# Masked attention with residual norms on one core: the other work of each step cut into smaller pieces and ordered by due date, with one output bank

## The chip, the cores and the metric

The kernel runs on one core of a Trainium2 chip, as one launch. The metric is the device time of that launch in microseconds. The core's engines are TensorE (PE in the profile), VectorE (DVE), ScalarE (ACT), GpSimd (POOL) and SyncE (SP), which here only issues DMAs. Each engine works through its own instructions in order and waits for the others by semaphores.

## The reference

There are eight frames of 2048 rows and 256 channels, one 0/1 matrix `adj` of 2048 x 2048 for all of them, and 8 heads of 32 channels:

```python
q, k, v = split(x @ w_qkv)                       # per frame: 2048 x 256 each, 8 heads of 32
scores = where(adj > 0, q @ k.T / sqrt(32), -1e9)
t = softmax(scores) @ v
y = layernorm(x + t)
z = layernorm(y + relu(y @ w1 + b1) @ w2 + b2)
out = layernorm(x + z)
```

Everything is float32.

## The kernel before, in words

The scores are held transposed: 128 keys on the partitions, queries along the free dimension. Work is cut into **items** `(f, qc, g, mb)`: frame f of 8, query chunk qc of 4 (512 queries), group g of 2 (4 heads), key block mb of 16 (128 keys). There are 1024 items, 128 in a frame, and 16 successive ones with the same `(f, qc, g)` form a group that sums into one output bank.

The main loop (L535) takes one **step** for each item t. In a step it issues, in this order: other work (`advance`, L449), the exponentials of item t+1 on ACT (L229), the scores of item t+2 (L222: four heads side by side in the rows of PE's array) with the addition of the mask on VectorE (L225, two halves of 128 x 1024), the values of item t (L241: four heads side by side in the columns), and the sum over keys (`add_up`, L256). The scores use three pairs of PSUM banks in turn, two pairs an item. The exponentials of a group are added up for the softmax's denominator: two chains of items by accumulating DMAs that POOL issues (L260; items 1, 4, 7, 10 and 2, 5, 9, 12), the rest by additions on POOL (L263), item 14 alone. POOL waits in its queue until the DMA before in the same chain has landed.

Two further banks, `x0` and `x1`, are left. Before the change they swap roles with each group: one takes the group's output, the other is the only bank for **other work**. This is everything on PE that isn't scores or values, written as generators:

- `turn`: load a chunk of the next frame's rows, transpose it, store it to a DRAM tile `xd`, and make its queries.
- `project`: reload such a chunk and make its keys and its values for one g.
- `denominator`: sum the four terms over the partitions (L299), transpose the result, take its reciprocal.
- `outcome`, then `tail`: divide the output and add x; normalize (`norm`: statistics on VectorE, a power on POOL that yields `nb`, and the scaling on ACT, L281), feed forward (two transposed banks, w1, w2), normalize, add x, normalize, store.

A generator yields `BANK` when it wants the other bank, `MORE` between the two halves of what it puts there, `HOLD` to be continued in the next step, or a number of steps to wait. `advance` continues the holder of the bank by one half a step, or gives the bank to the entry of `fill` with the earliest due step. If another entry is late, or in a group's last step, the holder runs on to its end. In a group's first step nothing of this is done. The table `NEXT` (L475) says in which step of a frame `turn` and `project` of the next frame are started. The reloads come through three tiles named `in`, by DMAs in SP's queue. A piece of `in_columns` with 512 columns (L53) is 8 instructions on PE.

Of the kernel before, what the change touches and what calls it, by code (L numbers as in the profile page):

```python
# [29 lines left out]
BANK, MORE, HOLD, TURNED, ROOM, INPUTS = -1, -2, -3, -4, -5, -10  # L30
# [30 lines left out]
def fast_path(ctx, tc, cst, x, adj, out, RS):  # L61
# [8 lines left out]
    kp = ctx.enter_context(tc.tile_pool(name="kp", bufs=2 * NCK + 2))  # L70
    qp = ctx.enter_context(tc.tile_pool(name="qp", bufs=2 * NCK + 2))
    vp = ctx.enter_context(tc.tile_pool(name="vp", bufs=2 * NCK + 2))
# [12 lines left out]
    state = {"pair": 0, "side": None, "turn": 0, "turned": False, "holder": None, "tails": 0}  # L85
# [65 lines left out]
    def turn_rows(xc, xT):  # L151
        for a in range(2):
            yield BANK
            ps = bank()
            for j in range(TPC):
                nc.tensor.transpose(ps[:, j * P:(j + 1) * P], xc[:, j, a * P:(a + 1) * P], ident)
            nc.scalar.copy(xT[:, a, :], ps)


    def turn(f, c):  # L160
        yield INPUTS - 2
        xc, xT = take([P, TPC, C], F32), take([P, 2, CH], F32)
        nc.sync.dma_start(xc, x[f, c * CH:(c + 1) * CH, :].rearrange("(j p) c -> p j c", p=P))
        yield 3
        yield from turn_rows(xc, xT)
        give(xc)
        yield 1
        nc.sync.dma_start(XD[f][c], xT)
        XT[f, c] = xT
        yield from queries(f, c, xT)  # L170
        give(xT)

    def channels(store, pool, name, key, xT, k0):
        yield BANK
        ps = bank()
        for a in range(2):
            if a:
                yield MORE
            in_columns(nc, ps, wqkv[:, a, k0:k0 + P], xT[:, a, :], start=(a == 0), stop=(a == 1))
        store[key] = pool.tile([P, CH], F32, name=name)  # L180
        nc.scalar.copy(store[key], ps)  # L181

    def reload(f, c):
        while (f, c) not in XT:
            yield 1
        yield INPUTS - 1
        xT = take([P, 2, CH], F32)
        nc.sync.dma_start(xT, XD[f][c])
        yield 3
        return xT  # L190

    def project(f, c, g, xT=None):
# [7 lines left out]
        for j in range(TPC):  # L200
            if j == TPC // 2:
                yield MORE
            for a in range(2):
                in_columns(nc, ps[:, j * P:(j + 1) * P], xT[:, a, j * P:(j + 1) * P],
                           wqkv[:, a, 2 * C + g * P:2 * C + (g + 1) * P], start=(a == 0), stop=(a == 1))
# [81 lines left out]
    def denominator(f, qc, g):  # L287
# [6 lines left out]
        for n, term in enumerate(terms):  # L294
            if n == 2:
                yield HOLD
# [8 lines left out]
        for j in range(TPC):  # L305
            nc.tensor.transpose(ps[:, j * P:(j + 1) * P], dT[:, j::TPC], ident)
# [21 lines left out]
    def divide(f, qc, y):  # L328
        rc = RC.pop((f, qc))
        for gg in range(2):  # L330
# [3 lines left out]
            for j in range(TPC):  # L334
                nc.tensor.transpose(ps[:, j * P:(j + 1) * P], oT[:, j::TPC], ident)
# [57 lines left out]
    def feed_forward(y):  # L393
# [3 lines left out]
        for a in range(2):  # L397
            yield BANK
            ps = bank()
            for j in range(TPC):  # L400
                nc.tensor.transpose(ps[:, j * P:(j + 1) * P], y[:, j, a * P:(a + 1) * P], ident)
# [6 lines left out]
        for d in range(2):  # L408
            yield BANK
            ps = bank()  # L410
            for a in range(2):
                if a:
                    yield MORE
                in_columns(nc, ps, w1s[:, a, d * P:(d + 1) * P], yT[:, a, :], start=(a == 0), stop=(a == 1))
# [4 lines left out]
        for jj in range(0, TPC, 2):  # L419
            yield BANK  # L420
            ps = bank()
            for j in range(jj, jj + 2):
                if j > jj:
                    yield MORE
                for d in range(2):
                    in_columns(nc, ps[:, (j - jj) * C:(j - jj + 1) * C], hT[:, d, j * P:(j + 1) * P], w2s[:, d, :],
                               start=(d == 0), stop=(d == 1))
# [13 lines left out]
    def resume(e, t):  # L441
        e[2] = next(e[1], None)
        state["holder"] = e if e[2] in (MORE, HOLD) else None if state["holder"] is e else state["holder"]
# [5 lines left out]
    def advance(t, free=True, finish=False):  # L449
        inputs = True  # L450
        if state["holder"]:
            free = False
            resume(state["holder"], t)
        for e in list(fill):
            while e[2] is not None and e[0] <= t and e is not state["holder"]:
                if e[2] == BANK:
                    if not free:
# [9 lines left out]
        late = any(e[2] == BANK and e[0] <= t for e in fill)  # L467
        while state["holder"] and (finish or late and state["holder"][2] == MORE):
            resume(state["holder"], t)

    items = [(f, qc, g, mb) for f in range(F) for qc in range(NCK) for g in range(2) for mb in range(MB)]
    LEAD = 2


    NEXT = {(1, 1): [(turn, 0)], (3, 1): [(turn, 1)], (3, 10): [(project, 0, 0)], (5, 1): [(turn, 2)],  # L475
            (5, 8): [(project, 1, 0)], (6, 0): [(turn, 3)], (6, 4): [(project, 2, 0)], (6, 8): [(project, 3, 0)],
            (6, 12): [(project, 0, 1)], (7, 0): [(project, 1, 1)], (7, 4): [(project, 2, 1)], (7, 8): [(project, 3, 1)]}

# [46 lines left out]
    def ask(f, c):  # L525
        xT = yield from reload(f, c)
        yield from queries(f, c, xT)
        give(xT)

    for _ in begin():  # L530
        pass
    for c in range(1, NCK):
        start(0, ask(0, c), 2 * MB * c - LEAD - 1)
    state["side"] = 0
    for t, (f, qc, g, mb) in enumerate(items):  # L535
        if mb == 0 and t:
            state["side"] = 1 - state["side"]
        if g == 1 and mb % 2 and (f + 1 < F or qc + 1 < NCK):
            load_mask(f + (qc + 1) // NCK, (qc + 1) % NCK, mb // 2)
        if f + 1 < F:  # L540
            for what, *which in NEXT.get((2 * qc + g, mb), []):
                due = t + MB // 2 if what is turn else items.index((f + 1, 0, which[1], which[0] * TPC)) - LEAD - 1
                start(t, what(f + 1, *which), due)
# [3 lines left out]
        if mb:  # L547
            advance(t, finish=mb == LAST)
# [12 lines left out]
        if mb == LAST:  # L561
            start(t + SUM, denominator(f, qc, g), t)
# [241 lines left out]
```

## Time and profile before

| | us |
|---|---|
| median of 3 runs | 3399.78 (3391.83 to 3401.1) |
| the profiled execution | 3399.32 |
| its span, first to last instruction | 3397.4 |
| PE busy | 3133.4 |
| POOL busy | 2595.8 |
| DVE busy | 2736.3 |
| ACT busy | 2431.0 |
| first exponentials of the main loop start at | 63.5 |

The mean granted clock of TensorE is 0.981 of full speed. Busy time is the time in which at least one instruction of the engine runs; for PE it is modelled, so that a busy PE need not be at its peak. In a line of the timeline stand the start in us, the duration, the engine, the line of the program, the operation, what it writes and reads, the number of instructions, and in brackets the idle time of the engine before it with what ended it. In a table of windows stand the window, its length, and for each engine its busy time with the number of instructions, then the granted clock and the DMA engines' busy share with what they moved in GB/s. In a list of waits stand who waited for whom, the sum, how often, and the longest.

### The profile page before, as it was taken

What the parts mean: (1) busy time and instruction counts of PE and PEld (TensorE: products, weight loads), DVE (VectorE), ACT (ScalarE), POOL (GpSimd) and SP (SyncE); (2) the same over time, 40 slices, a digit from 0 to 9 for tenths busy, and PEclk for the clock granted to TensorE, in tenths of its full rate; (3) what the DMA queues carried; (4) which work ended last, traced back from release to release, by engine and by line L of the source; (5) the groups of instructions that cost most, each with busy time, mean ns of one, the idle gap of its engine ahead of it and who ended that gap; (6) DMA issues with size and microseconds to landing.
All of it is one profiled execution on the core that took longest, in us unless ns stands there. A gap on an engine that the chain in (4) does not pass through costs nothing. (4 is left out here: it accounts for less than half of the span.)

```text
span 3397.4 us, 68228 instructions
## 1 busy us (share of the span) xinstructions
PE 3133.4 (92%) x28948; PEld 978.7 (29%) x28948; DVE 2736.3 (81%) x3203; ACT 2431.0 (72%) x1937; POOL 2595.8 (76%) x1357
## 2 busy tenths in 40 slices
PE   7899999989999999989999999999999989998884
PEld 4222233222332223222332223322233222332221
DVE  4788878878788887878888788887888877888884
ACT  3677777767677777777777677777777767777773
POOL 0577778787787877877878787887887877788884
PEclk8899999999999999999999999999999999999997
DMA  9678778778688787778787778778788778777773
GB/s 309 141 162 179 167 175 183 156 151 201 149 179 172 160 182 175 169 148 187 171 174 169 159 173 191 152 168 177 166 185 174 157 159 181 175 164 160 160 151 82
DMA packets 149352, 576.88 MB, mean 170 GB/s; under 512 B 14608, under 2 KB 67344, under 8 KB 99888
## 3 DMA queue, kind: packets, MB, share of 16 engines
q0 software_dynamic: 64560, 435.85, 63.9%
q1 hardware_dynamic: 83664, 135.30, 11.9%
q8 instruction: 229, 3.75, 0.4%
q10 hardware_dynamic: 816, 1.31, 0.1%
q14 instruction: 83, 0.68, 0.1%
HBM read 131.99 MB, written 37.75 MB: 50 GB/s over the span
## 5 line engine op out<-in xcount | busy, mean ns | idle before, releaser
L225 DVE TENSOR_TENSOR p<-s,mask 128x1024 f32<-128x1024 f32 x2048 | 2410.1, 1218 | 530.6 <-PE s L222 331.6
L229 ACT ACTIVATE p<-p 128x2048 f32<-128x2048 f32 x1024 | 1956.2, 1910 | 517.8 <-DVE p L225 438.1
L263 POOL TENSOR_TENSOR p<-p 128x2048 f32<-128x2048 f32 x382 | 1828.0, 4806 | 245.4 <-ACT p L229 240.2
L222 PE MATMUL s<-qT,kT 32*128 32x512 f32 x8192 | 1176.3, 644 | 133.2 <-DVE p L225 127.6
L241 PE MATMUL x<-p,v 128*32 128x512 f32 x8192 | 1096.8, 607 | 23.7 <-ACT p L229 23.7
L260 POOL DMA_DIRECT2D p<-p x384 | 364.3, 1016 | 443.7 <-DMA p<-p 241.2
L222 PEld LDWEIGHTS s<-qT,kT 32*128 32x128 f32 x8192 | 321.8, 184 | 774.8 <-DVE p L225 724.2
L241 PEld LDWEIGHTS x<-p,v 128*32 128x32 f32 x8192 | 161.6, 108 | 807.5 <-issue 287.9
L53 PE MATMUL x<-in,wqkv 128*32 128x512 f32 x1888 | 242.5, 603 | 29.9 <-DMA in<-xd 29.0
L281 ACT ACTIVATE y<-y,nb,rs 128x256 f32<-128x256 f32 x372 | 219.4, 591 | 61.8 <-POOL nb L278 61.8
L299 PE MATMUL x<-p,ones 128*32 128x512 f32 x2016 | 239.3, 592 | 0.0
L270 DVE BATCH_NORM_STATS2 st<-y 128x6 f32<-128x256 f32 x372 | 155.2, 417 | 6.3 <-DMA y<-in_x_dram 6.3
L53 PE MATMUL x<-turned,w1s 128*32 128x512 f32 x992 | 123.2, 603 | 5.0 <-ACT hT L415 4.9
L301 ACT COPY dT<-x 128x512 f32<-128x512 f32 x63 | 36.9, 585 | 125.6 <-PE x L299 125.6
L53 PE MATMUL x<-w2s,hT 128*32 128x256 f32 x2048 | 123.8, 382 | 0.4 <-ACT hT L415 0.4
L53 PEld LDWEIGHTS x<-wqkv,in 128*32 128x32 f32 x3584 | 101.0, 110 | 46.1 <-issue 31.4
L53 PEld LDWEIGHTS x<-in,wqkv 128*32 128x32 f32 x1888 | 61.3, 111 | 176.0 <-issue 149.5
L53 PE MATMUL x<-wqkv,in 128*32 128x128 f32 x3584 | 111.9, 273 | 0.0
L299 PEld LDWEIGHTS x<-p,ones 128*32 128x32 f32 x2016 | 65.5, 110 | 150.8 <-issue 150.8
L275 POOL TENSOR_TENSOR rs<-rs,mhalf 128x4 f32<-128x4 f32 x93 | 97.1, 1044 | 7.7
L53 PEld LDWEIGHTS x<-w2s,hT 128*32 128x32 f32 x2048 | 67.0, 111 | 73.2 <-issue 37.5
L181 ACT COPY kT<-x 128x512 f32<-128x512 f32 x59 | 34.5, 585 | 73.3 <-PE x L53 72.7
(117 smaller groups left out, 1421.5 us busy)
## 6 DMA issues: line engine op xcount, KB each, us to landing
p<-p POOLq DMA_DIRECT2D x384, 1024.0 KB, 10.4
mask<-md SPq DMA_DIRECT2D x248, 128.0 KB, 7.3
y<-in_x_dram POOLq DMA_DIRECT2D x62, 512.0 KB, 5.8
in<-xd SPq DMA_DIRECT2D x59, 512.0 KB, 10.7
p<-in_adj_dram SPq DMA_DIRECT2D x16, 1024.0 KB, 9.7
out_dram<-y SPq DMA_DIRECT2D x31, 512.0 KB, 2.9
in<-in_x_dram SPq DMA_DIRECT2D x29, 512.0 KB, 9.1
xd<-in SPq DMA_DIRECT2D x28, 512.0 KB, 8.4
```

Of the source, the lines that this page charges most:

```text
L53: nc.tensor.matmul(out[r:r + D], lhsT[:, r:r + D], rhs, start=start, stop=stop)
L222: nc.tensor.matmul(ps2[half][:, j, :], KT[f, mb // TPC, g][r:r + D, (mb % TPC) * P:(mb % TPC + 1) * P], QT[f, qc, g][r:r + D, :], start=Tr ...
L225: nc.vector.tensor_tensor(pt[:, 2 * half:2 * half + 2, :], ps, MK[f, qc, mb // 2][:, mb % 2, None, :].to_broadcast([P, 2, CH]), ALU.add)
L229: nc.scalar.activation(PT[item], PT[item], AF.Exp, scale=1.0 / math.sqrt(D))
L241: nc.tensor.matmul(O[grp][r:r + D, :], V[f, mb // TPC, g][:, mb % TPC, r:r + D], PT[item][:, h, :], start=(mb == 0), stop=(mb == LAST))
L260: nc.gpsimd.dma_start(PT[f, qc, g, chain[0]], PT.pop(item), accum_op=ALU.add)
L263: nc.gpsimd.tensor_tensor(first, first, PT.pop(item), ALU.add)
L270: nc.vector.bn_stats(st, t[:, j, :])
L275: nc.gpsimd.tensor_tensor(rs, rs, cst["mhalf"], ALU.pow)
L281: nc.scalar.activation(t[:, j, :], t[:, j, :], AF.Identity, bias=nb[:, j:j + 1], scale=rs[:, j:j + 1])
L299: nc.tensor.matmul(ps[r:r + D, :], cst["ones"], term[:, h, :], start=(n == 0), stop=(n == len(terms) - 1))
L301: nc.scalar.copy(dT, ps)
```

## The change

Other work is metered. Each call of `advance` adds a credit of 2200, kept at most at 2200, and each piece takes 4 for each of its columns (2048 for 512 columns), a transposed bank 1400. A piece is issued if at least 1024 are left, or if the earliest entry that could use the bank is due. The halves become smaller: values yield `MORE` after each of four column blocks, the denominator after each of its four terms. The forced end in a group's last step and the rest in its first step are dropped. `WAIT` replaces `HOLD`: the denominator starts two steps after its group instead of four, but its last term is held until the fourth.

Queries are no longer made in `turn`. A generator `ask` reloads the chunk and makes them, for the same frame in steps 2, 34 and 66 (chunks 1 to 3) and for the next frame's chunk 0 in step 66. The other entries of `NEXT` move too, and reloads wait five steps instead of three before they are used. There are 12 tiles for keys and for values instead of 10, and 6 for queries instead of 10. `state["side"]` stays 0: output always goes to `x0`, and other work to `x1`.

```diff
-BANK, MORE, HOLD, TURNED, ROOM, INPUTS = -1, -2, -3, -4, -5, -10
+BANK, MORE, WAIT, TURNED, ROOM, INPUTS = -1, -2, -3, -4, -5, -10
+STEP, UNIT, TURN, KEPT = 2200, 1024, 1400, 2200
...
-    kp = ctx.enter_context(tc.tile_pool(name="kp", bufs=2 * NCK + 2))
-    qp = ctx.enter_context(tc.tile_pool(name="qp", bufs=2 * NCK + 2))
-    vp = ctx.enter_context(tc.tile_pool(name="vp", bufs=2 * NCK + 2))
+    kp = ctx.enter_context(tc.tile_pool(name="kp", bufs=3 * NCK))
+    qp = ctx.enter_context(tc.tile_pool(name="qp", bufs=6))
+    vp = ctx.enter_context(tc.tile_pool(name="vp", bufs=3 * NCK))
...
+    def columns(out, lhsT, rhs, start, stop):
+        state["credit"] -= 4 * out.shape[-1]
+        in_columns(nc, out, lhsT, rhs, start, stop)
+
+    def transposes(ps, src, ident=ident):
+        state["credit"] -= TURN
+        for j, s in enumerate(src):
+            nc.tensor.transpose(ps[:, j * P:(j + 1) * P], s, ident)
...
         nc.sync.dma_start(xc, x[f, c * CH:(c + 1) * CH, :].rearrange("(j p) c -> p j c", p=P))
-        yield 3
+        yield 5
         yield from turn_rows(xc, xT)
         give(xc)
         yield 1
         nc.sync.dma_start(XD[f][c], xT)
         XT[f, c] = xT
-        yield from queries(f, c, xT)
         give(xT)
...
         nc.sync.dma_start(xT, XD[f][c])
-        yield 3
+        yield 5
         return xT
...
         for j in range(TPC):
-            if j == TPC // 2:
+            if j:
                 yield MORE
...
         for n, term in enumerate(terms):
-            if n == 2:
-                yield HOLD
+            if n:
+                yield MORE
+            while n == len(terms) - 1 and state["now"] < ready:
+                yield WAIT
+            state["credit"] -= 4 * CH
...
-    def advance(t, free=True, finish=False):
+    def advance(t, finish=False):
+        state["credit"] = min(max(state["credit"], 0) + STEP, KEPT)
+        state["now"] = t
+        free = not state["holder"]
+
+        def more():
+            if state["holder"] and state["holder"][2] == WAIT:
+                return False
+            due = [e[3] for e in fill if e[2] == BANK and e[0] <= t or e is state["holder"]]
+            return finish or state["credit"] >= UNIT or min(due) <= t
+
+        if state["holder"]:
+            resume(state["holder"], t)
+            while state["holder"] and more():
+                resume(state["holder"], t)
         inputs = True
-        if state["holder"]:
-            free = False
-            resume(state["holder"], t)
         for e in list(fill):
             while e[2] is not None and e[0] <= t and e is not state["holder"]:
                 if e[2] == BANK:
-                    if not free:
+                    if not free or not more():
                         break
...
-        late = any(e[2] == BANK and e[0] <= t for e in fill)
-        while state["holder"] and (finish or late and state["holder"][2] == MORE):
-            resume(state["holder"], t)
+            while e is state["holder"] and more():
+                resume(e, t)
...
-    NEXT = {(1, 1): [(turn, 0)], (3, 1): [(turn, 1)], (3, 10): [(project, 0, 0)], (5, 1): [(turn, 2)],
-            (5, 8): [(project, 1, 0)], (6, 0): [(turn, 3)], (6, 4): [(project, 2, 0)], (6, 8): [(project, 3, 0)],
-            (6, 12): [(project, 0, 1)], (7, 0): [(project, 1, 1)], (7, 4): [(project, 2, 1)], (7, 8): [(project, 3, 1)]}
+    NEXT = {1: [(turn, 0)], 2: [(ask, 1)], 20: [(turn, 1)], 34: [(ask, 2)], 40: [(project, 0, 0)], 50: [(turn, 2)],
+            60: [(project, 1, 0)], 66: [(ask, 0), (ask, 3)], 72: [(turn, 3)], 80: [(project, 2, 0)], 92: [(project, 3, 0)],
+            100: [(project, 0, 1)], 104: [(project, 1, 1)], 108: [(project, 2, 1)], 112: [(project, 3, 1)]}
...
-    for c in range(1, NCK):
-        start(0, ask(0, c), 2 * MB * c - LEAD - 1)
     state["side"] = 0
     for t, (f, qc, g, mb) in enumerate(items):
-        if mb == 0 and t:
-            state["side"] = 1 - state["side"]
...
-        if mb:
-            advance(t, finish=mb == LAST)
+        if t:
+            advance(t)
...
         if mb == LAST:
-            start(t + SUM, denominator(f, qc, g), t)
+            start(t + 2, denominator(f, qc, g, t + SUM), t + SUM + 4)
```

The calls of `in_columns` and the loops of transposes in the generators now go through `columns` and `transposes`.

## The prediction

> **What bounds the kernel now.** I read the page first (busy shares), then the timeline in two ordinary stretches, then the table of windows over one of the eight frames, then the list of waits. The page:
>
> ```profile
> PE 3133.4 (92%) x28948; PEld 978.7 (29%) x28948; DVE 2736.3 (81%) x3203; ACT 2431.0 (72%) x1937; POOL 2595.8 (76%) x1357
> ```
>
> No engine is far from full, so the average settles nothing. I went to the timeline, where the first score matmul (L222) of each step is the clock tick. First without other work between values (L241) and the next scores, then with one piece (L53, x8) and with two (x16); of the lines, only PE's are shown:
>
> ```profile
> 1450.59 1.14 PE L222 MATMUL s<-qT,kT 32*128 32x512 f32 x8 [0.35 <-DVE p L225]
> 1451.65 1.07 PE L241 MATMUL x<-p,v 128*32 128x512 f32 x8
> ...
> 1453.13 1.14 PE L222 MATMUL s<-qT,kT 32*128 32x512 f32 x8 [0.41 <-DVE p L225]
> ```
>
> ```profile
> 1606.61 1.14 PE L222 MATMUL s<-qT,kT 32*128 32x512 f32 x8
> ...
> 1608.57 1.04 PE L53 MATMUL x<-in,wqkv 128*32 128x512 f32 x8
> ...
> 1609.54 1.14 PE L222 MATMUL s<-qT,kT 32*128 32x512 f32 x8
> ...
> 1611.49 1.90 PE L53 MATMUL x<-turned,w1s 128*32 128x512 f32 x16
> ...
> 1613.32 1.14 PE L222 MATMUL s<-qT,kT 32*128 32x512 f32 x8
> ```
>
> The empty step takes 2.54 us and PE waits 0.35 to 0.41 us in it for VectorE; one piece takes 2.93 us, two take 3.78 us, both without a gap on PE. So a step is bound by the larger of two things: a loop of VectorE's first half and the scores (about 2.5 us), or PE's own sum: scores 1.07, values 1.00 and 0.86 a piece. I took the distance between first score matmuls for 1020 of the 1024 steps and sorted them by the other work on PE in between: empty, median 2.55 us; one transposed bank 2.75; one piece 2.93; two pieces 3.78. These four medians times their counts give 3113.6 us of the 3223.4 us that the steps take. The missing 109.8 us are stalls in a few places. The windows of frame 3 (its 16-step groups) show one:
>
> ```profile
> 1361.94:1409.33 47.39, 46.56 (x424) 14.18 (x420) 40.79 (x51) 39.05 (x33) 39.11 (x24) 1.00 0.78 170
> ...
> 1458.23:1515.79 57.56, 48.54 (x373) 13.06 (x373) 42.82 (x52) 38.34 (x31) 45.91 (x26) 0.94 0.83 179
> ```
>
> The first group has PE busy 46.56 of 47.39 us; the second loses about 9 us and TensorE's granted clock falls to 0.94. The timeline there, and the waits:
>
> ```profile
> 1506.43 1.94 PE L53 MATMUL x<-in,wqkv 128*32 128x512 f32 x8 [7.24 <-DMA in<-xd]
> 1508.29 1.93 PE L222 MATMUL s<-qT,kT 32*128 32x512 f32 x8
> ```
>
> ```profile
> POOL p L260 <- DMA p<-p: 241.2, 63, 8.1
> ...
> ACT y L281 <- POOL nb L278: 61.8, 20, 9.4
> ```
>
> PE waits in its own queue for a reloaded tile, and runs the next 3.9 us at half pace. The last wait is the other kind: ScalarE, in order, stands behind POOL, which itself waits for an accumulating DMA.
>
> **The Trainium skill.** "Perfetto Trace Analysis", section Optimization Strategy: where the most-contended engine changes over time, interleaving the regimes can help. The trace agrees that there are two regimes, VectorE's 2.55 us and PE's 3.78 us. The same page, section Matmuls: independent matmul groups should rotate through PSUM banks so that an eviction overlaps the next group; the change goes against it for the output bank, priced below. "TensorE: Matmul & The Clock Gate", Part 1: PE falls to half clock after an idle window of about 3.4 us; the 1.93 us scores after 7.24 us of idling, against 1.14, agree. The same page, Architectural detail: ScalarE and VectorE are strict FIFO, which the wait for nb shows.
>
> **The change, part by part.**
>
> Spreading. From the order in which both programs issue PE's instructions I counted the steps by kind (1023 steps). Before: 245 empty, 243 with a transposed bank, 226 with one piece, 309 with two. After: 63, 243, 590, 127. The 844 pieces are the same work (226 + 618 = 590 + 254). So 182 empty steps and 182 double ones become 364 single ones: 182 x (2.55 + 3.78 - 2 x 2.93) = 182 x 0.47 = 85.5 us. PE's idle time in an empty step hides about half of a piece (2.55 + 0.86 would be 3.41, and it is 2.93); that is all there is to win here. Doubles remain because the feed-forward pieces (w1, w2) are past their due step when they get their turn. The steps then cost 3113.6 - 85.5 = 3028.1 us.
>
> Earlier loads. Before, the reload planned in step 58 is first read in step 61, 3 steps of about 2.9 us, while such a reload took 10.7 us at the median and 21.6 at most. Steps 61 and 62 are over their medians by 2.0, 2.4, 6.1, 9.1, 8.1, 6.5 and 8.0 us in frames 0 to 6: 42.2 us. After, I counted from load to first read at least 5 steps (105 to 110) and otherwise 6 to 28, 15 us and more. I take the 42.2 us as gone. If only half of a late load is covered, 20 us stay.
>
> Late queries. Each of the 32 chunks but the very first is now reloaded for its queries, where 3 were before: 28 loads of 512 KB more, each 0.3 to 1.2 us of issue on SP, which only issues and mostly waits. By the page SP's queue moved 135.3 MB in 11.9% of the DMA engines' time, so 14.7 MB more are 1.3%, on top of 78%. Nothing waits for these but the queries, which load 10 steps ahead or more; that lead hides them, and without it each would cost what step 61 did, about 6 us. I take 0, from 0 to 20. Behind a load in SP's queue stand the mask pieces; their next reading is over ten steps away.
>
> Buffers. Keys and values get 12 tiles, queries 6: 30 in all as before. A key tile written in step 111 falls on one that was last read in step 97. Nothing.
>
> One output bank. values' first matmul of a group now waits for the copy oT of the group before; behind it on PE stand the other work and the scores of the step after, and behind those VectorE. In the trace oT ended 0.66 to 2.22 us after the last values matmul (mostly 0.87 to 1.44). The next values follow 1.93 us after it where a piece lies between (0.86 + 1.07), and about 1.43 us where none does (groups starting at steps 48 and 80). So most groups wait nothing; at worst 2.22 - 1.43 = 0.8 us in all 64, 51 us; nothing can be gained by it. I take 0.1 us, 6 us. On the other side the first step of a group, never used for other work before, is now used; that is in the counts.
>
> Denominators. They begin two steps after the group instead of four, one term a step; a chain's sum is read one step earlier, the pool's sum in the same step. Before, PE never waited there (idle before L299: 0.0). In frame 3 POOL issues the last chained add 14 or 15 steps into the group, and it lands 10.4 us (3.5 steps) later, against a reading in step 19: half a step to a step and a half of slack. A wait there holds up PE in order, so the next scores. 0 to 1 us in 64 groups; I take 0.
>
> Less slack. 286 of the 590 single steps also carry VectorE work, mostly the statistics of 0.42 + 0.18 us: 2.36 + 0.60 makes 2.96 to 2.99 us against 2.93. Up to 0.06 x 286 = 17 us, hidden by the steps without; I take 8. The other 67.6 us of stalls (y's division on VectorE about 0.7 us four times a frame, nb about 3 us a frame) I leave as they are, from 30 to 110.
>
> The sum: 3028.1 + 67.6 + 6 + 8 = 3109.7 us of steps, plus 174.0 us outside them (3397.4 - 3223.4, start-up and end, unchanged): span 3283.7 us. The profiled execution took 1.9 us over its span and the median of the runs lies 0.5 us above it: 3286 us, 3.4% below 3399.8. A difference of 0.3% is about what a measurement of this kernel can tell from none.
>
> **Rivals.**
> (1) All scattered stalls shrink too, since nb is now issued in step 60 instead of 61, 90 instead of 92 and 121 instead of 124, with one chained add fewer ahead of it on POOL: 3028 + 25 + 174 + 2 = 3229 us. For it: the 61.8 us of waits behind nb. Against it: POOL has less idle time.
> (2) VectorE or ScalarE becomes the bound. If each step paid its largest engine sum without any help from its neighbours (VectorE 2.40 plus its extras, ScalarE 1.95 plus its extras, PE as above), the steps would take 3167 us: 3343 us. Against it: by the same rule the steps before would take 3268 us and took 3223 with the load stalls.
> (3) Slower: POOL takes over. A group of frame 3 holds 325.5 / 8 = 40.7 us of POOL work, and 241.2 / 64 = 3.8 us of waiting for chained DMAs, 44.5 in all, against 48.4 us a group in my sum. Steps of 3.0 us instead of 3.2 bring a chain's adds 0.6 us closer, four waits a group: 46.9. It decides from 50.4 us a group (3223 / 64), that is, if the waits grow to 9.7 us; at 10 us it is 64 x 50.7 + 174 + 2 = 3421 us. Against it: the group of 47.39 us above ran with 39.11 us of POOL work and no stall, and frame 7 keeps 47 us for several groups.
> (4) The spread does not reach the path: only the loads' 42 us come back, 3357 us. The gapless 2.93 and 3.78 us steps speak against it.
>
> **How the numbers follow.** Sum as worked 0.60 (3255 to 3315), rival 1 0.15, rivals 2 and 4 0.14, rival 3 0.08, no change to speak of 0.03. The range takes the first, most of rival 1 and half of 2: 3232 to 3345 us. Faster 0.88, same 0.03, slower 0.09.
>
> **What would show it.** Right: distances of first score matmuls with the same medians and the new counts; PE busy near 96%; the wait of L53 for the reload gone; granted clock 0.99. Wrong: single steps over 3.05 us at the median; idle time before the denominator's matmuls; values waiting for oT; longer waits behind nb or for chained DMAs on POOL.

## The result, and the profile after

The changed kernel takes 3281.12 us (median of 4 runs, 3279.45 to 3283.31), 0.9656 of the kernel before, with a 95% interval of 0.9639 to 0.9673. The forecast was 3286 us. The profiled execution took 3279.45 us with a span of 3277.3 us, at a mean granted clock of 0.983 (before: 0.981). In the changed kernel the line numbers move: scores L230, mask L233, exponentials L237, values L249, chained DMAs L268, POOL's additions L271, nb L286, the scaling of y L289, denominators L310, pieces of `in_columns` L54.

The first part of the page, busy time by engine:

```profile
PE 3112.2 (95%) x28948; PEld 979.2 (30%) x28948; DVE 2737.7 (84%) x3203; ACT 2438.8 (74%) x1937; POOL 2591.2 (79%) x1357
```

Every engine has the number of instructions it had before, so nothing was taken out. The span is 120 us shorter: PE is idle for 99 us less, and its busy time is 21 us shorter. The timeline of three steps with one piece each, PE's lines only:

```profile
1282.97 1.14 PE L230 MATMUL s<-qT,kT 32*128 32x512 f32 x8
1284.04 1.07 PE L249 MATMUL x<-p,v 128*32 128x512 f32 x8
1284.92 1.04 PE L54 MATMUL x<-in,wqkv 128*32 128x512 f32 x8
1285.89 1.14 PE L230 MATMUL s<-qT,kT 32*128 32x512 f32 x8
1286.97 1.06 PE L249 MATMUL x<-p,v 128*32 128x512 f32 x8
1287.85 1.04 PE L54 MATMUL x<-in,wqkv 128*32 128x512 f32 x8
1288.82 1.14 PE L230 MATMUL s<-qT,kT 32*128 32x512 f32 x8
```

The two halves that the kernel before put into one step of 3.78 us stand in two steps of 2.93 us, without a gap on PE. Sorted as in the prediction (distances of first score matmuls, here over the same 1021 steps of both traces; the sums take the four medians of the kernel before for both kernels):

| steps | before: count, median us | after: count, median us |
|---|---|---|
| without other work | 245, 2.55 | 63, 2.54 |
| one transposed bank | 243, 2.75 | 243, 2.74 |
| one piece | 225, 2.93 | 588, 2.93 |
| two pieces | 308, 3.78 | 127, 3.79 |
| sum of medians | 3116.5 | 3031.8 |
| stalls over the medians | 109.8 | 75.9 |
| outside the steps | 171.1 | 169.6 |
| span | 3397.4 | 3277.3 |

So the span fell by 84.7 us from the kinds of steps, 33.9 from stalls, and 1.5 outside them. The windows of frame 3 of the changed kernel, its fourth group (in which the kernel before lost about 9 us to the reload) and its last:

```profile
1404.13:1449.47 45.34, 44.86 (x408) 13.67 (x404) 41.73 (x52) 35.65 (x29) 36.41 (x23) 1.00 0.95 221
...
1596.08:1647.74 51.66, 48.79 (x481) 15.39 (x477) 42.30 (x52) 39.47 (x33) 44.38 (x26) 0.97 0.88 203
```

The last group in the kernel before:

```profile
1666.66:1718.49 51.83, 50.72 (x509) 16.04 (x509) 42.89 (x52) 38.88 (x33) 42.77 (x25) 1.00 0.82 188
```

The fourth group is now nearly gapless on PE, at full clock. The last has PE idle for 2.9 us, 1.1 before, and a lower clock: a stall that the kernel before did not have there. The list of groups and the list of waits of the changed kernel show what went and what came:

```profile
L249 PE MATMUL x<-p,v 128*32 128x512 f32 x8192 | 1097.6, 608 | 14.0 <-ACT p L237 14.0
...
L310 PE MATMUL x<-p,ones 128*32 128x512 f32 x2016 | 262.8, 598 | 4.3 <-POOL p L271 2.7 <-DMA p<-p 1.6
L54 PE MATMUL x<-in,wqkv 128*32 128x512 f32 x1888 | 244.0, 594 | 4.0 <-DMA in<-xd 4.0
```

```profile
POOL p L268 <- DMA p<-p: 94.4, 36, 6.1
...
DVE p L233 <- DMA p<-p: 49.0, 35, 3.1
...
ACT y L289 <- POOL nb L286: 37.1, 10, 9.3
```

Two lines from the list of waits of the kernel before:

```profile
PE x L53 <- DMA in<-xd: 29.0, 8, 7.2
...
DVE p L225 <- DMA p<-p: 13.6, 9, 3.1
```

PE's wait for a reload fell from 29.0 to 4.0 us (one wait, at step 112 of frame 0). Values never wait for the output's copy `oT`. POOL's own waits for chained DMAs fell from 241.2 to 94.4 us, ScalarE's behind nb from 61.8 to 37.1 us. What grew is VectorE's wait for a p tile that a chained DMA still holds: 49.0 us, 13.6 before. Of the 49.0 us, 33 stand at steps 23, 81 and 115. The timeline at step 115 of frame 3, VectorE's and PE's lines:

```profile
1607.70 1.04 PE L310 MATMUL x<-p,ones 128*32 128x512 f32 x8
1609.55 2.36 DVE L233 TENSOR_TENSOR p<-s,mask 128x1024 f32<-128x1024 f32 x2 [2.30 <-DMA p<-p]
1610.83 1.29 PE L230 MATMUL s<-qT,kT 32*128 32x512 f32 x8 [2.09 <-DVE p L233]
...
1612.04 1.94 PE L249 MATMUL x<-p,v 128*32 128x512 f32 x8
```

VectorE can't write the masked scores before a p tile is free; PE's next scores wait for the score banks that VectorE should have emptied, and the values after it take 1.94 us in place of 1.07. The record of the granted clock shows half speed for 3.4 us from 1611.7 us on.

### The profile page after: what moved, and what is told of

Its sections match the earlier page's. It is cut to its first block, busy times and chain, and to the rows that moved or that the text cites. A ratio compares the mean times of both kernels' runs of the same rounds, so it can differ in the third digit from the quotient of the medians.

```text
span 3277.3 us, 68323 instructions
## 1 busy us (share of the span) xinstructions
PE 3112.2 (95%) x28948; PEld 979.2 (30%) x28948; DVE 2737.7 (84%) x3203; ACT 2438.8 (74%) x1937; POOL 2591.2 (79%) x1357
## 5 line engine op out<-in xcount | busy, mean ns | idle before, releaser
L233 DVE TENSOR_TENSOR p<-s,mask 128x1024 f32<-128x1024 f32 x2048 | 2409.4, 1218 | 395.7 <-PE s L230 190.0
L237 ACT ACTIVATE p<-p 128x2048 f32<-128x2048 f32 x1024 | 1956.2, 1910 | 554.8 <-DVE p L233 486.8
L271 POOL TENSOR_TENSOR p<-p 128x2048 f32<-128x2048 f32 x382 | 1824.0, 4776 | 268.5 <-ACT p L237 266.2
L230 PE MATMUL s<-qT,kT 32*128 32x512 f32 x8192 | 1173.5, 642 | 70.2 <-DVE p L233 65.7
L249 PE MATMUL x<-p,v 128*32 128x512 f32 x8192 | 1097.6, 608 | 14.0 <-ACT p L237 14.0
L268 POOL DMA_DIRECT2D p<-p x384 | 360.0, 955 | 289.4 <-DMA p<-p 94.4
L230 PEld LDWEIGHTS s<-qT,kT 32*128 32x128 f32 x8192 | 321.1, 183 | 679.0 <-DVE p L233 632.4
L249 PEld LDWEIGHTS x<-p,v 128*32 128x32 f32 x8192 | 161.5, 108 | 795.2 <-issue 294.2
L310 PE MATMUL x<-p,ones 128*32 128x512 f32 x2016 | 262.8, 598 | 4.3 <-POOL p L271 2.7
L54 PE MATMUL x<-in,wqkv 128*32 128x512 f32 x1888 | 244.0, 594 | 4.0 <-DMA in<-xd 4.0
L289 ACT ACTIVATE y<-y,nb,rs 128x256 f32<-128x256 f32 x372 | 219.1, 590 | 37.1 <-POOL nb L286 37.1
L54 PE MATMUL x<-w2s,hT 128*32 128x256 f32 x2048 | 123.9, 383 | 3.2 <-DVE y L436 2.1
L54 PE MATMUL x<-turned,w1s 128*32 128x512 f32 x992 | 122.9, 592 | 0.2
L54 PEld LDWEIGHTS x<-wqkv,in 128*32 128x32 f32 x3584 | 102.3, 110 | 62.8 <-issue 59.8
L54 PE MATMUL x<-wqkv,in 128*32 128x128 f32 x3584 | 117.0, 273 | 0.0
L310 PEld LDWEIGHTS x<-p,ones 128*32 128x32 f32 x2016 | 65.7, 111 | 160.3 <-issue 145.8
L54 PEld LDWEIGHTS x<-in,wqkv 128*32 128x32 f32 x1888 | 61.3, 110 | 145.8 <-issue 112.1
L54 PEld LDWEIGHTS x<-w2s,hT 128*32 128x32 f32 x2048 | 66.4, 111 | 77.0 <-issue 30.0
L414 POOL TENSOR_TENSOR y<-y,be1b2r 128x1024 f32<-128x1024 f32 x32 | 85.5, 2671 | 0.6
L355 POOL TENSOR_TENSOR y<-y,g2r 128x1024 f32<-128x1024 f32 x31 | 82.3, 2656 | 1.8 <-ACT y L289 1.8
## 6 DMA issues: line engine op xcount, KB each, us to landing
p<-p POOLq DMA_DIRECT2D x384, 1024.0 KB, 10.5
in<-xd SPq DMA_DIRECT2D x87, 512.0 KB, 10.6
```

The lines of the kernel that those rows point to most:

```text
L54: nc.tensor.matmul(out[r:r + D], lhsT[:, r:r + D], rhs, start=start, stop=stop)
L230: nc.tensor.matmul(ps2[half][:, j, :], KT[f, mb // TPC, g][r:r + D, (mb % TPC) * P:(mb % TPC + 1) * P], QT[f, qc, g][r:r + D, :], start=Tr ...
L233: nc.vector.tensor_tensor(pt[:, 2 * half:2 * half + 2, :], ps, MK[f, qc, mb // 2][:, mb % 2, None, :].to_broadcast([P, 2, CH]), ALU.add)
L237: nc.scalar.activation(PT[item], PT[item], AF.Exp, scale=1.0 / math.sqrt(D))
L249: nc.tensor.matmul(O[grp][r:r + D, :], V[f, mb // TPC, g][:, mb % TPC, r:r + D], PT[item][:, h, :], start=(mb == 0), stop=(mb == LAST))
L268: nc.gpsimd.dma_start(PT[f, qc, g, chain[0]], PT.pop(item), accum_op=ALU.add)
```

## The experiments

All ratios are to the kernel before in the same batch, with 95% intervals.

| run | median us | ratio |
|---|---|---|
| before, one reload earlier | 3380.21 | 0.995 (0.9938 to 0.9963) |
| before, one output bank | 3399.82 | 1.0021 (1.0007 to 1.0035) |
| after, ten key and value tiles | 3277.18 | 0.9654 (0.9629 to 0.968) |
| after, no metering | 3472.4 | 1.0223 (1.0196 to 1.025) |
| after, no metering, sums late | 3389.56 | 0.9984 (0.9975 to 0.9993) |
| after, queries early | 3297.82 | 0.9717 (0.9698 to 0.9735) |
| after, twelve p tiles | 3255.86 | 0.959 (0.9576 to 0.9603) |
| and tail due four steps later | 3267.4 | 0.9615 (0.96 to 0.963) |
| and denominators due two later | 3402.97 | 1.0028 (1.0017 to 1.0039) |
| after, four POOL extras a group | 3382.52 | 0.9959 (0.9941 to 0.9977) |
| after, eight POOL extras a group | 3515.4 | 1.0351 (1.0331 to 1.0371) |
| after, reloads twice | 3328.99 | 0.9798 (0.9778 to 0.9818) |

**The late reload alone.** The kernel before, with one entry of the table moved six steps ahead:

```diff
-    NEXT = {(1, 1): [(turn, 0)], (3, 1): [(turn, 1)], (3, 10): [(project, 0, 0)], (5, 1): [(turn, 2)],
+    NEXT = {(1, 1): [(turn, 0)], (3, 1): [(turn, 1)], (3, 4): [(project, 0, 0)], (5, 1): [(turn, 2)],
```

> The kernel before, with one entry of NEXT moved: the first project of the next frame is started in step 52 of a frame instead of 58, so that its reload runs 8 steps ahead of its first reading instead of 3. Nothing else changes but a few pieces of work (316 double steps instead of 309, 3 us). The sum of my prediction: the stall of steps 61 and 62 goes, 42 us less, 3361 us (3352 to 3370), and the wait of PE for the reload falls from 29.0 us to under 5. Rival, that late loads with their half-clock tail are most of the whole gain of 119 us: 3320 us or less. Rival, that PE would wait for something else in that place: 3390 to 3400 us.

Measured: 3380.21 us, 0.5% faster, not 1.1%: above the expected range, and below the rival's 3390. The wait for the reload is gone from PE, but a stall of 3.6 to 5.7 us stands at step 65 in five frames. The timeline of this run there, ScalarE's scaling and PE:

```profile
1902.35 1.14 PE L222 MATMUL s<-qT,kT 32*128 32x512 f32 x8 [0.41 <-DVE p L225]
...
1903.99 0.60 ACT L281 ACTIVATE y<-y,nb,rs 128x256 f32<-128x256 f32 x1 [5.35 <-POOL nb L278]
...
1907.02 1.14 PE L241 MATMUL x<-p,v 128*32 128x512 f32 x8 [3.53 <-ACT p L229]
```

The scaling waits for nb, the exponentials stand behind it on ScalarE, and PE's values wait for those. In the kernel before this stall appears in one frame only, frame 1 (6.5 us at step 65), and that is where the reload was hardly late (2.4 us against 6 to 9 in frames 2 to 6). The traces show why. In frames 1 to 6, nb is written 11.9 to 16.5 us after the end of step 60 in the kernel before and 12.6 to 14.9 us after it here, so POOL is about as late in both. But the next four steps took 18.3 to 21.3 us in frames 2 to 6 with the late reload, and take 13.0 us without it: PE and ScalarE now get there before nb does. So about half of the 42.2 us is paid either way.

**One output bank alone.** The kernel before, without the swap:

```diff
-        if mb == 0 and t:
-            state["side"] = 1 - state["side"]
```

> The kernel before with one line pair less: the two spare banks no longer swap roles, output always goes to x0. The first step of a group holds no other work here, so the copy oT has only the next scores to hide behind. The sum: the eighth of the groups whose oT ended 2.2 us after the last values waits 0.8 us, the two eighths with 1.45 us wait 0.1 us, the rest nothing: 8 us more, 3408 us (3400 to 3415). Rival, that the first values of every group wait for the copy: 0.6 us and more in all 64 groups, 3440 us or more.

Measured: 1.0021, which is 7 us with an interval of 2 to 12. The group of values in the list of groups, in this run and then in the kernel before:

```profile
L241 PE MATMUL x<-p,v 128*32 128x512 f32 x8192 | 1096.6, 607 | 27.4 <-ACT oT L245 14.7 <-ACT p L229 12.7
```

```profile
L241 PE MATMUL x<-p,v 128*32 128x512 f32 x8192 | 1096.8, 607 | 23.7 <-ACT p L229 23.7
```

No first step of a group holds other work in this run, yet the values wait for `oT` in only ten of them: the eight at step 96 and two at step 64. In the same ten places the kernel before waited for the exponentials, so the idle time before the values grew by 3.7 us and not by 14.7. In the profiled execution steps 61 and 62 also lie 52.0 us over their medians, 42.2 in the kernel before; nothing in the edit explains that part. In the changed kernel no values wait for `oT`. In 45 of its 63 changes of group a piece or a transposed bank stands on PE between the last values of one group and the first of the next. In the other 18, most of them at steps 48 and 80, only the scores stand there, and the copy is still in time, by 0.06 to 0.44 us.

**The key and value tiles.**

```diff
-    kp = ctx.enter_context(tc.tile_pool(name="kp", bufs=3 * NCK))
...
-    vp = ctx.enter_context(tc.tile_pool(name="vp", bufs=3 * NCK))
+    kp = ctx.enter_context(tc.tile_pool(name="kp", bufs=2 * NCK + 2))
+    vp = ctx.enter_context(tc.tile_pool(name="vp", bufs=2 * NCK + 2))
```

> The changed kernel with 10 tiles for keys and 10 for values instead of 12. The order of all instructions stays the same; only what the copies kT and v have to wait for changes. The sum priced the two more tiles at nothing: 3281 us, within 5. Rival, that they let the next frame's keys and values be made early without waiting for the last scores and values of this one: ScalarE's copies wait, 10 us or more on top.

Measured: 3277.18 us, no difference from the changed kernel. The tiles are worth nothing, and their room is free for something else.

**No metering.**

```diff
-STEP, UNIT, TURN, KEPT = 2200, 1024, 1400, 2200
+STEP, UNIT, TURN, KEPT = 4400, 1024, 1400, 4400
```

> The changed kernel with the meter opened: STEP and KEPT 4400 instead of 2200, so that both pieces of a bank go into one step, as before. All the rest of the change stays. Steps by kind: 293 empty, 243 with a transposed bank, 126 single, 361 double, against 63, 243, 590 and 127. The sum: 3149 us of step medians against 3038, with the same stalls, so 111 us more than the changed kernel: 3392 us (3375 to 3405). Rival, that the gain came from the loads, the due dates and the end of the forced finish, and not from the spreading: within 20 us of the changed kernel, 3261 to 3301 us.

Measured: 3472.4 us, 80 over the expectation, slower than the kernel before. The kinds of steps came as counted (medians 3141.6, 110 over the changed kernel), but the stalls grew from 75.9 to 174.7 us. Of these, 108 us sit at steps 18, 50, 82 and 114, three steps after the last item of a group. The list of waits of this run:

```profile
PEld x L310 <- DMA p<-p: 140.1, 47, 9.1
...
PE x L310 <- DMA p<-p: 99.9, 35, 8.2
```

The denominator begins two steps after the last item. Unmetered, it puts two terms on PE in that step and the third in the next, a step earlier than the meter lets it. Nearly all of PE's waits (33 of the 35, 98 us) stand before the third term, the sum of the second chain, which the chained DMAs have not finished. The expectation had counted pieces and not asked when their operands are ready.

**No metering, denominators as late as before.** In addition to the last edit:

```diff
-            start(t + 2, denominator(f, qc, g, t + SUM), t + SUM + 4)
+            start(t + SUM, denominator(f, qc, g, t + SUM), t + SUM + 4)
```

> The changed kernel without the metering (a whole bank of credit in every step) and with the denominators started four steps after their group, as in the kernel before, instead of two. Steps by kind: 356 with no piece, 243 with a transposed bank, 424 with two pieces; by the medians 141 us more than the changed kernel. Theory: the surplus of the run without the metering (3472 where the steps' kinds gave 3392) came from denominators that were put ahead of their chained DMA additions; started later they do not wait, the excess falls from 174.7 to about 80 us, and the time is 3281 + 141 = 3422 (3405 to 3440), below the run without the metering although its kinds of steps are 30 us dearer. Rival: the surplus belongs to the pairing of pieces itself (double steps let the other engines fall behind): then it stays and the time is 3500 or more.

Measured: 3389.56 us, 83 below the run without metering although its steps are dearer by kind. The denominators' line in the list of groups:

```profile
L310 PE MATMUL x<-p,ones 128*32 128x512 f32 x2064 | 245.4, 593 | 1.8 <-DMA p<-p 1.1 <-ACT oT L253 0.7
```

The waits for the chained DMAs are all but gone, the stalls are 62.8 us, fewer than in the changed kernel: pairing pieces does not by itself let other engines fall behind. The time is under the expected range because the stalls fell lower than expected and because 12 us less lie outside the steps. All of that is after the last step, where 60.5 us pass here, 59.9 in the run before this one and 72.3 in the changed kernel; why is not known. Against this run the metering is worth 108 us (its steps by kind: 139). Against the kernel before, this run is only 0.2% faster: its kinds of steps are 55 us dearer, and fewer stalls and the shorter end make up for little more than that.

**Queries early.** The changed kernel, queries made in `turn` again:

```diff
         XT[f, c] = xT
+        yield from queries(f, c, xT)
         give(xT)
...
-            if to < F:
+            if to < F and (what is not ask or to == 0 and which[0]):
```

with ten key, value and query tiles.

> The changed kernel with the queries projected right after the transposes of their rows, as in the kernel before (28 fewer reloads of 512 KB; ten key, value and query tiles, as before). Steps by kind: 51 with no piece, 243 with a transposed bank, 621 with one, 101 with two, 7 with three; by the medians 5.5 us less than the changed kernel. Theory (late queries cost nothing by themselves, their loads lie under other work): 3276 (3268 to 3288). Rival: the 28 loads crowd the DMA engines beside the chained additions and hold p tiles longer; without them VectorE's waits for a p tile fall from 49 us to under 30, and the time is 3255 or less. Rival on the other side: the queries that stand early push other pieces into the crowded first third of a group, and the time is over 3295.

Measured: 3297.82 us, 17 slower, although its steps were to be 5.5 us cheaper by kind. That is the last rival's range. The second group of frame 3 in the windows of this run, and a line from its waits:

```profile
1311.59:1369.92 58.33, 52.73 (x548) 17.89 (x544) 41.98 (x52) 39.93 (x34) 46.39 (x25) 0.94 0.80 175
```

```profile
DVE p L234 <- DMA p<-p: 81.5, 39, 4.3
```

That group takes 58.3 us, 50.2 in the changed kernel. By the order in which PE's instructions are issued, the queries push what follows: the denominator gets the bank in step 22 instead of 21, and three of its four terms come due together in step 23, instead of two. That step takes 7.07 us, the p tiles come free late, and steps 22 to 25 lose 5.6 to 9.1 us over their medians in frames 1 to 6. The loads made no difference that can be seen: the rival that they crowd out the chained DMAs found no support, since with 28 loads less VectorE waited longer for p tiles, not less. The order of the pieces changed with them, so this run alone does not settle it.

**Reloads twice.** Each reload issued twice into the same tile:

```diff
         nc.sync.dma_start(xT, XD[f][c])
+        nc.sync.dma_start(xT, XD[f][c])
```

> The changed kernel with each reload of 512 KB issued twice into the same tile (87 loads and 44.6 MB more; extra work, nothing left out). The late queries of the change brought 28 such loads. Theory (they lie under other work on the 16 DMA engines, which are near 80% busy): nothing from the loads' bytes as such, at most a few chained additions that land a step later: 3281 to 3292. Rival: loads and chained additions share the DMA engines at the limit, every load costs the chain that is under way its own time (2 to 3 us of all engines) and p tiles come free later: 87 x 0.7 us or more, 3340 and over, and then the 28 loads of the change cost about 20 us.

Measured: 3328.99 us, 48 slower, so neither as expected nor for the rival's reason. Two lines from its waits:

```profile
POOL p L269 <- DMA p<-p: 93.1, 43, 5.3
...
PE x L54 <- DMA in<-xd: 60.3, 7, 15.7
```

POOL's waits for chained DMAs are where they were (94.4), and VectorE's for p tiles are 36.1 us, fewer than the changed kernel's 49.0. The loss is seven late reloads, at step 110 in frames 1 to 6 and step 112 in frame 0: 60.3 us of waiting on PE, for which the stalls at 115 and 116 went, some 19 us. The second copy writes the same tile and was issued only when the first had landed: in frame 4 the first left at 2066.4 us, the second left at 2077.1 and landed at 2086.2. That is 19.8 us in place of some 10.6, the changed kernel's median for a reload, and five steps are about 15. The edit thus doubled the latency and not only the bytes. What it shows: the bytes are not seen in the waits for chained DMAs and p tiles, and a load that is longer than its lead is felt, 60.3 us of waiting for 48 us of time.

**A twelfth p tile.** The two key tiles and two value tiles that were worth nothing make room for one more p tile:

```diff
-    kp = ctx.enter_context(tc.tile_pool(name="kp", bufs=3 * NCK))
...
-    vp = ctx.enter_context(tc.tile_pool(name="vp", bufs=3 * NCK))
-    pp = ctx.enter_context(tc.tile_pool(name="pp", bufs=11))
+    kp = ctx.enter_context(tc.tile_pool(name="kp", bufs=2 * NCK + 2))
+    vp = ctx.enter_context(tc.tile_pool(name="vp", bufs=2 * NCK + 2))
+    pp = ctx.enter_context(tc.tile_pool(name="pp", bufs=12))
```

> The changed kernel with twelve p tiles instead of eleven, and ten key and ten value tiles to make room for it (the run with ten key and value tiles, 3277 us, is its baseline). Theory: the new stalls at steps 81, 115 and 23 of a frame are VectorE waiting for a free p tile that a chained DMA still holds (49.0 us of its waits in the changed kernel, 13.6 before); one tile more gives every allocation a step more, so that row should fall below 15 us and the stalls at 81, 115 and 23 (about 5 us in each of six frames, 30 us) should go: 3247 us (3240 to 3260). Rival: the tile is only the last of several things that come late there (POOL's additions and its DMA issues are behind as well), the wait is then put down to another releaser, and the time stays at 3277 (3270 to 3281).

Measured: 3255.86 us, 25 below the changed kernel and 21 below the run with ten key and value tiles, in the expected range. VectorE's list of waits:

```profile
DVE p L233 <- DMA p<-p: 3.9, 5, 1.3
```

49.0 us became 3.9. The stalls at 23, 81 and 115 are gone, some came at 83 to 85 (1.4 to 5 us a frame, where PE now waits for the denominator's last terms: 18.1 us before L310, 4.3 in the changed kernel), and all stalls together fell from 75.9 to 53.1. The key and value tiles were worth nothing by themselves, so the p tiles were the cause of the new stalls. This version beats both kernels.

**Due dates moved further.** On top of twelve p tiles, the tail due four steps later; and then also the denominators two steps later:

```diff
-        start(begin + 10, tail(f, qc, y, xin), begin + 26)
+        start(begin + 10, tail(f, qc, y, xin), begin + 30)
...
-            start(t + 2, denominator(f, qc, g, t + SUM), t + SUM + 4)
+            start(t + 2, denominator(f, qc, g, t + SUM), t + SUM + 6)
```

> The run with twelve p tiles (3256 us), and the tail alone may take its pieces four steps later; the denominators stay where the changed kernel has them. Steps by kind: 51 with no piece, 237 with a transposed bank, 639 with one piece, 77 with two, 13 with three and 6 with two and a bank; by the medians 5.7 us less. Theory: what made the run with both edits slow (3403) was the denominators' later last piece, which holds four p tiles longer and pushes the division and the residual DMA towards the norm that reads it (VectorE waited 69.4 us for that DMA and 57.6 us for p tiles there); without it both waits stay under 10 us, and the time is 3250 (3244 to 3260). Rival: the later tail did it (norm, feed-forward and the second norm run into the next tail), and the time is 3290 or more.

> As the run with twelve p tiles, and in addition the tail may take its pieces four steps later and the denominators' last piece is due two steps later, so that more pieces stand alone: 44 steps with no piece, 243 with a transposed bank, 642 with one, 87 with two and 7 with four, against 63, 243, 590, 127 and none. By the steps' medians that is 8.8 us less. Theory (a step's price depends on the work in it, not on which work it is): 9 us under the run with twelve p tiles, so 3238 (3228 to 3252). Rival: denominators that hold four p tiles two steps longer eat the twelfth tile: the waits of VectorE for a p tile come back, and the time is at or above the run with twelve p tiles, 3250 to 3280.

Measured: 3267.4 us with the first, 3402.97 with both. The first has 50 double steps fewer, worth 5.6 us by the medians as counted, but its time over the medians is 66.6 us against 53.1, at steps 10, 65 and 96; neither expectation had that. At step 10 this is less a stall than a price: two pieces and a transposed bank in one step took 6.27 us in six frames, and had been counted at about 4.4. With both edits the time is 136 us more again. Two lines from the waits of that run:

```profile
DVE st L278 <- DMA y<-in_x_dram: 69.4, 14, 6.2
...
DVE p L233 <- DMA p<-p: 57.6, 28, 3.8
```

The statistics of the tail stand in VectorE's queue at a fixed step. With the denominator two steps later the division and the residual DMA are later as well, and VectorE waits in order for that DMA (steps 80 and 112, 3.8 to 5.8 us each), the masks behind it; at step 67, ScalarE's wait for nb costs another 6 to 8 us a frame. Without the later denominators the line of the residual DMA is at 6.2 us, one wait after the last step that the changed kernel has too, and the p tiles' line is at 7.9 us. Both are what the expectation gave to the denominators; the tail's part, 12 us, was missed. The later denominators without the later tail were not run.

**More work on POOL.** The changed kernel with 11 key tiles and 4 or 8 multiplications more in each group, on a tile of their own:

```diff
         f, qc, g, mb = item
+        if mb in EXTRA:
+            nc.gpsimd.tensor_tensor(idle, idle, idle, ALU.mult)
```

> The changed kernel with four more GpSimd multiplications of 128 x 512 in each group of 16 steps, on a tile that nothing else reads (extra work, nothing left out; 11 key tiles to make room). By the additions' 4.8 us for four times the size, about 1.2 us each, 4.8 us in a group. Theory (GpSimd's work and waits fill 44.5 us of a group that takes 48.6): 49.3 us fits in most groups, and only the groups that are shorter than that are held up: 3281 + 10 to 45, so 3290 to 3325. Rival (GpSimd is already what sets the spread steps): all of it shows, 64 x 4.8 = 307 us, 3590. Other rival (GpSimd has much more room): 3281 (up to 3287).

> The same with eight more multiplications in each group, about 9.6 us. Theory: 44.5 + 9.6 = 54.1 us of a group, over the 48.6 that PE needs, so GpSimd sets the time of a group: 3281 + 64 x 5.5 = 3630 (3500 to 3700), and the surplus over the run with four is several times as large as that run's own. Rival (GpSimd has room, its waits shrink as it gets busier): under 3350. Rival (it is the bound already): 3281 + 614 = 3895.

Measured: 3382.52 and 3515.4 us. Neither the limit per group nor either rival. POOL's busy time rose by 261.4 and 519.6 us, the time by 101 and 234 us: 0.39 and 0.45 us for each added one, already with four. The group of extras in the run with eight, and two of its waits:

```profile
L271 POOL TENSOR_TENSOR idle<-idle 128x512 f32<-128x512 f32 x512 | 726.9, 1420 | 3.9
```

```profile
DVE p L233 <- DMA p<-p: 183.9, 92, 6.6
...
ACT y L295 <- POOL nb L292: 133.7, 38, 10.4
```

With none, four and eight extras VectorE's wait for p tiles is 49.0, 80.7 and 183.9 us, ScalarE's for nb 37.1, 70.3 and 133.7. POOL is not the bound, for then all of it would show. The extras did not slow the others' own instructions either: VectorE's busy time is 2737.7, 2739.8 and 2740.2 us, ScalarE's 2438.8, 2438.4 and 2438.0. But POOL hands out what the others need, p tiles by its chained DMAs and nb, and where it comes a few us later in a crowded place, they wait, though it is idle for 11% of the span even with eight extras.

## Why the prediction was right, point by point

The forecast gain was 113.7 us: 85.5 from spreading and 42.2 from the loads, less 14 for the bank and the slack. Measured were 118.6 us: 84.7 from the kinds of steps, 33.9 from stalls. The first term is the mechanism and came as worked out. That the rest came near is in part luck, as the points show.

- **Spreading, -85.5 us.** Measured -84.7 us: the four medians stayed within 0.01 us and the counts came as worked out. Taking the metering away raised the sum by the kinds of steps by 110 us, and the time by 108 us in the run that kept the denominators off their unfinished sums. This is the core of the gain, and shown.
- **Earlier loads, -42.2 us.** The wait went as said. As a price it was too high: alone it is worth 17 us (0.5%), because nb's delay at step 65 had been hidden under it. The step that failed is "I take the 42.2 us as gone", which priced a wait and did not ask what was late next. In the changed kernel that place costs little (step 64, 1.2 to 2.2 us in frames 1 to 6, 7.6 in frame 7). There nb is written 8.6 to 9.5 us after the end of step 60 in frames 1 to 6, 12.6 to 14.9 in the run with the earlier reload alone, as rival 1 had said of nb; that this is the reason was not tested by itself.
- **Late queries, 0.** Their loads cost nothing that the runs show. But the step missed a gain: made early they cost 17 us, mostly in the second group of a frame.
- **Buffers, 0.** Right: 3277.18 us with ten tiles.
- **One output bank, +6.** 0 in the changed kernel: its copy is in time in every group, also in those without other work in between, so that nothing is left of the 0.1 us a group. In the kernel before the ratio says +7, but the trace gives only 3.7 us of it to the values, nearly all at step 96, where the expectation had its latest copies; that the ratio agrees with the sum is in part luck. One reading was short: the latest copy ended 5.86 us after the last values, not 2.22.
- **Denominators, 0.** Right for PE, 4.3 us of waiting. It is the metering that makes it so: without it the early start costs 83 us over the late one. What the step did not ask is how long the terms' p tiles are held: the last term is read 6.2 steps after a group's last item on average, 5.5 before.
- **Less slack, +8.** Not seen: nine in ten single steps are at or below 2.94 us.
- **The other stalls, 67.6.** With bank and slack the prediction had 81.6 us in all, and 75.9 were measured, but they are others. y's division and much of nb's waiting went; p tiles came, 36 us over the medians at steps 23, 81 and 115 and the steps after them. That size was luck. The wrong sign that I had named, longer waits for chained DMAs on POOL, did not come: they fell there, and rose on VectorE. A p tile is held from the masks to the landing of its DMA, and steps of 2.93 us in place of 3.78 take tiles faster than a landing of 10.5 us gives them back; and the denominators hold their four tiles later than before. That the tiles ran short is shown by the twelfth; how much of it comes from either reason is not.
- **Rivals.** (1) did not come by itself; 23 of its 43 us of stalls were to be had with one more p tile. (2) did not come: the steps with one piece kept PE's 2.93 us. (3) was rightly put aside, but its form was wrong: it let POOL's work and its waits for chained DMAs grow to 50.4 us a group at no cost, and with the extras they were 46.3 and 49.8 us a group while the time rose by 101 and 234 us. (4) fell with the gapless steps of 2.93 us.
- **The clock** rose to 0.983, not 0.99. In the changed kernel's record of the granted clock 111.5 us are at half speed (131.8 before). Only 27.3 of them lie in the steps (44.4 before); the other 84.2 lie before the first step and after the last, where the kernel before had 87.4. Without any in the steps the mean would be 0.987.

## What to carry to other kernels

Where steps alternate between two bounds, move work from the full ones to the empty ones and price it by the step medians of each kind: the sum came true within a microsecond here. But a due date moves buffers too: before starting something earlier or later, ask when its operands are ready, which tiles it holds, and which instruction with a fixed place in an in-order queue reads its result. A stall's length is not what its removal pays; a second one often lies hidden under it, and a unit with idle time can still cost through the moment at which it delivers.

## What was not expected of the hardware

The extras on POOL took 1.03 to 2.60 us, median 1.35 us, for 128 x 512 elements; a quarter of the 4.8 us that 128 x 2048 take is 1.2. TensorE lost pace after shorter pauses than the 7.24 us of the prediction. In the steps of the changed kernel and of the run with eight extras together, the next eight values matmuls after a pause on PE took over 1.4 us in place of 1.07 in none of 48 cases after 0.5 to 1 us, in 6 of 50 after 1 to 2 us, in 12 of 28 after 2 to 3 us, and in 23 of 28 after 3 to 6 us. The record of the granted clock shows what made them slow: all 44 slow values of the two traces overlap a stretch at half speed, and in the steps such a stretch lasts 3.4 us or a multiple of it. So already a stall of 2 us can cost some of itself again in slow matmuls. Why one pause of 2 us is followed by such a stretch and another is not was not tested. The accumulating DMAs of 1 MB landed in 10.3 to 11.0 us at the median in all runs, also where reloads were issued twice (10.7).
